# A four-layer graph attention kernel: layer 0's means and deviations made one batch ahead, on ACT and POOL

## The chip, the cores and the metric

The kernel runs on one core of a Trainium2 chip. The metric is the time of one execution on the device in microseconds. Before the change it is 2933.27 us, the median of three runs (2932.54 to 2933.4); the profiled execution spans 2931.4 us. Five engines work side by side, each with a queue of its own: TensorE (PE; its weight loads are listed as PEld), VectorE (DVE), ScalarE (ACT), GpSimd (POOL) and SyncE (SP, which here issues transfers).

## The reference

There are 16 batches; each is a graph of 1024 nodes with 256 features in fp32 and an adjacency matrix. Four layers follow one another, each on the output of the one before. Every layer starts with a layer norm over the features of each node and a relu, and then computes graph attention with a residual:

```python
def _layernorm(x, axis=-1, eps=1e-5):
    m = jnp.mean(x, axis=axis, keepdims=True)
    v = jnp.var(x, axis=axis, keepdims=True)
    return (x - m) / jnp.sqrt(v + eps)
```

Layers 0 to 2 have one head of 256 features: the normed and rectified features are multiplied by a matrix W, each edge gets a leaky-relu score from two dot products with a vector a, the scores are masked by the adjacency and put through a softmax, and the features of the neighbours are summed with these weights. Layers 1 and 2 pass the sum through an elu. Layer 3 has four heads of 64 features and a layer norm of its own inside each head.

For the change only the first step of layer 0 matters: the mean and the deviation of the 256 features of each input node. They depend on the input x alone.

## The kernel before

**Tiles.** A batch's features lie in SBUF as a tile x_b of 128 partitions by 8 node tiles by 256 features. The eight node tiles are treated in four pairs. In the listing P is 128, NI is 8, D is 256, B is 16 and HALF is 512.

**From features to V.** `project` (L315) makes one pair ready for the attention. It needs the means and the reciprocal deviations. Batch 0's layer 0 takes them from DVE's bn_stats. All others have sums of the features: DVE turns a sum into a negative mean (L332), subtracts it and rectifies (L302), ACT squares the difference and adds the squares up (L309), and POOL adds a constant (L292) and raises to the power −1/2 (L293). PE transposes the centred features into a psum tile "misc" (L338; there are two such tiles), ACT copies them out as hT (L340; three buffers), PE multiplies them by W into an accumulator (L345), and an `evict` function scales the result by the reciprocal deviation into V (ACT at L413 and L415 or L433 and after, DVE at L417). In layers 1 to 3 the sums come for free from the residual addition before; in layer 0 the function `first` (L512) lets DVE sum the features up first (L517).

**Attention, layers 0 to 2.** `attend` runs it. `weigh` puts a row of scores on all partitions with PE (L374), and DVE makes eight tiles of edge weights from it (L367, one fused operation over 128 by 1024). `product` multiplies weights by V, eight matmuls of 257 columns for a node tile (L461). `finish` divides by the total (DVE L385 and L386), for layers 1 and 2 with an elu of two ACT passes (L393 and L395) and two DVE additions (L396 and L397), and the next layer's `project` follows for each pair.

**Layer 3.** For each of four heads, `weigh3` makes rows of scores (PE L574) and weights (DVE L367), and PE forms the sums and totals in blocks of 24 matmuls with 32-column operands (L586). ACT copies the two accumulators out (L663), PE transposes them (L670 and L678), DVE divides (L681), and `center` and `rescale` do the head's layer norm over POOL (L544, L561 and L562), DVE (L545 to L551, L555 and L560) and ACT (L553), again with POOL's L292 and L293. At each of the eight copies L663 one further step of two side tasks is taken: `next(testing)`, a check of the adjacency by ACT (L175), and `next(coming)`, the load of the batch two ahead.

**The load.** `load` (above L146) fetches the adjacency as bytes on POOL's queue. It then issues four transposing transfers of the mask on SP's queue, and after these the transfer of the 1 MB of x, also on SP's queue. x_b has three buffers.

**What sets the order.** Each batch is a Python generator; even batches form one stream, odd batches another, and a small loop runs the two with weights given by the `yield` values, so that one batch's layer 3 is interleaved with layers 1 and 2 of the other stream's batch. Within what this emits, a list scheduler sets the order of each engine's queue from estimated costs; instructions put under `tc.keep_in_program_order` keep their order among themselves. An engine then takes its queue as built.

Of the kernel before, what the change touches and what calls it, by code (L numbers as in the profile page):

```python
# [32 lines left out]
F32 = mybir.dt.float32  # L33
BF = mybir.dt.bfloat16
# [3 lines left out]
AF = mybir.ActivationFunctionType  # L38
ALU = mybir.AluOpType
AX = mybir.AxisListType  # L40

P = 128
# [3 lines left out]
LN_EPS = 1e-5  # L46
# [15 lines left out]
def short_path(ctx: ExitStack, tc: tile.TileContext, ins: dict, out: bass.AP, bad: bass.AP):  # L62

    nc = tc.nc
    x, adj = ins["x"], ins["adj"]
    B, N, D = x.shape
    H, T, E = ins["L3_a_src"].shape
    NI = N // P
# [19 lines left out]
    minus_half = const.tile([P, 1], F32, name="minus_half")  # L88
# [21 lines left out]
    xs, masks = {}, {}  # L110
# [3 lines left out]
    def fetch_nodes(b: int):  # L114
        xs[b] = nodes.tile([P, NI, D], F32, name="x_b")
        if b == 0:

            for c in range(NI // 2):
                nc.scalar.dma_start(
                    xs[b][:, ts(c, 2), :],  # L120
                    x[b, ts(c, 2 * P), :].rearrange("(p t) f -> p t f", t=2),
                )
            return
        fetch = nc.sync.dma_start(xs[b].rearrange("p (c t) f -> p c t f", t=2), in_blocks(x[b]))
        if b > 0:
            tc.keep_in_program_order(fetch)

    def load(b: int):


        narrow = narrows[b % 2]
        rows = narrow.bitcast(U8)
        if b == 0:

            for h in range(NH):
                for t in range(2):
                    cast = nc.gpsimd.dma_start(
                        halves[h].bitcast(U8).rearrange("(c t q) j -> t c q j", t=2, q=P)[t],
                        adj[b].rearrange("(c q t) j -> t c q j", t=2, q=P)[t, :, :, ts(h, HALF)],
                    )  # L140
                    tc.keep_in_program_order(cast)
        else:
            for c in range(NI // 2):
                cast = nc.gpsimd.dma_start(
                    rows.rearrange("(c t q) j -> c q t j", t=2, q=P)[c],
                    adj[b, ts(c, 2 * P), :].rearrange("(q t) j -> q t j", t=2),  # L146
                )
                tc.keep_in_program_order(cast)
        if b < 2:
            fetch_nodes(b)  # L150
        yield

        mask = masks[b] = nodes.tile([P, NI // 2, N, 2], U8, name="mask")
        for c in range(NI // 2):
            turn = nc.sync.dma_start_transpose(
                mask[:, c].rearrange("p n t -> p (n t)").bitcast(BF),
                halves[c // NH][:, ts(c % NH, P)] if b == 0 else narrow[:, ts(c, P)],
            )
            tc.keep_in_program_order(turn)
            yield  # L160
        if b > 1:
            fetch_nodes(b)
            yield

    def test(b: int):
# [17 lines left out]
    work = ctx.enter_context(tc.tile_pool(name="work", bufs=3))  # L183
# [6 lines left out]
    bias = const.tile([P, D], F32, name="bias")  # L190
# [98 lines left out]
    def inverse_root(squared: bass.AP, n: int, elements: int, eps: float, times=1.0) -> bass.AP:  # L289

        r = small.tile([P, max(n, NI) if n > 2 else n], F32, name=f"rstd{8 if n > 2 else n}")[:, :n]
        nc.gpsimd.tensor_scalar(r, squared, times, elements * eps, op0=ALU.mult, op1=ALU.add)  # L292
        nc.gpsimd.tensor_tensor(r, r, minus_half.to_broadcast([P, n]), op=ALU.pow)  # L293
        return r
# [1 line left out]
    def accumulator(b: int) -> bass.AP:  # L296
        return psum.tile([P, HALF], F32, name=f"acc{b % 2}")

    def center_by_sums(xb: bass.AP, minus_mean: bass.AP, pair: int, centered: bass.AP) -> bass.AP:

        for n in range(2):
            nc.vector.tensor_scalar(  # L302
                centered[:, n, :], xb[:, 2 * pair + n, :], minus_mean[:, n : n + 1], 0.0,
                op0=ALU.add, op1=ALU.max,
            )
        squared = small.tile([P, 2], F32, name="squared")
        for n in range(2):
            square = work.tile([P, D], BF, name="square", bufs=1)
            nc.scalar.activation(  # L309
                square, xb[:, 2 * pair + n, :], AF.Square, bias=minus_mean[:, n : n + 1],  # L310
                accum_out=squared[:, n : n + 1],
            )
        return inverse_root(squared, 2, D, LN_EPS)

    def project(b: int, l: int, xb: bass.AP, sums: bass.AP, pair: int, evict):  # L315


        centered = work.tile([P, 2, D], F32, name="centered", bufs=3)
        if sums is None:
            mv = small.tile([P, 2, nc.vector.BN_AGGR_DIM], F32, name="mv", bufs=2)  # L320
            for n in range(2):
                stats = small.tile([P, nc.vector.BN_STATS_DIM], F32, name="stats", bufs=1)
                nc.vector.bn_stats(stats, xb[:, 2 * pair + n, :])
                nc.vector.bn_aggr(mv[:, n, :], stats)
                nc.vector.tensor_scalar(  # L325
                    centered[:, n, :], xb[:, 2 * pair + n, :], mv[:, n, 0:1], 0.0,
                    op0=ALU.subtract, op1=ALU.max,
                )
            rstd = inverse_root(mv[:, :, 1], 2, D, LN_EPS, D)
        else:  # L330
            minus_mean = small.tile([P, 2], F32, name="minus_mean")
            nc.vector.tensor_scalar_mul(minus_mean, sums[:, ts(pair, 2)], -1.0 / D)  # L332
            rstd = center_by_sums(xb, minus_mean, pair, centered)
        yield 0.5
        turned = psum.tile([P, NK, 2 * P], F32, name="misc")
        for n in range(2):
            for k in range(NK):
                nc.tensor.transpose(turned[:, k, ts(n, P)], centered[:, n, ts(k, P)], ident)  # L338
        hT = wide.tile([P, NK, 2 * P], F32, name="hT", bufs=3)
        nc.scalar.mul(hT, turned, ROOT_D)  # L340
        yield 1.0
        for n in range(2):
            projected = accumulator(b)[:, : D + EXT[l]]
            for k in range(NK):
                nc.tensor.matmul(  # L345
                    projected, hT[:, k, ts(n, P)], W[l][:, k, :],
                    start=(k == 0), stop=(k == NK - 1),
                )
            evict(2 * pair + n, projected, rstd[:, n : n + 1])
        yield 2.5  # L350
# [48 lines left out]
        )  # L399

    def batch(b: int):
        xb = xs.pop(b)
        if b == 0:
            next(preparing)
        coming = load(b + 2) if b + 2 < B else iter(())
# [21 lines left out]
        def begin3():  # L427
            h3 = last["h3"] = single.tile([P, NI, D], F32, name="h3")
            V3 = nodes.tile([P, NI, H, E + 1], F32, name="V", bufs=4)
            ex = last["ex"] = small.tile([P, NI, 3 * H], F32, name="ex", bufs=2)  # L430

            def evict3(i: int, projected: bass.AP, rstd: bass.AP):
                nc.scalar.activation(ex[:, i, :], projected[:, D:], AF.Exp, scale=rstd)  # L433
                nc.scalar.mul(h3[:, i, :], projected[:, :D], rstd)
                q = ex[:, i, :H].unsqueeze(2)
                nc.gpsimd.tensor_mul(
                    V3[:, i, :, :E], h3[:, i, :].rearrange("p (h e) -> p h e", h=H),
                    q.to_broadcast([P, H, E]),
                )
                nc.gpsimd.tensor_copy(V3[:, i, :, E:], q)  # L440
                nc.gpsimd.tensor_add(xb[:, i, :], xb[:, i, :], beta)  # L441

            return V3, evict3
# [63 lines left out]
            add_elu(xb[:, i, :], acc, total)  # L507

        V, evict = begin(0)
        sums = small.tile([P, NI], F32, name="sums_of_x")  # L510

        def first(pair: int):  # L512
            if b == 0:

                yield from project(b, 0, xb, None, pair, evict)
                return
            nc.vector.tensor_reduce(sums[:, ts(pair, 2)], xb[:, ts(pair, 2), :], AX.X, ALU.add)  # L517
            yield from project(b, 0, xb, sums, pair, evict)

        pairs = [first(pair) for pair in range(NI // 2)]  # L520
        for n in range(NI // 2 + 2):
            for pair in range(max(n - 2, 0), min(n + 1, NI // 2)):
                yield from islice(pairs[pair], 1)
# [82 lines left out]
        def add_totals(h: int, j: int):  # L606
# [4 lines left out]
            ]  # L611
            in_tiles(parts, total, j == 2, j == NI - 4)

        behind = weigh3(0)
        yield from start(behind, b)

# [7 lines left out]
        for h in range(H):  # L624
# [36 lines left out]
            for accT in (acc, total) if h == 0 else (total, acc):  # L661
                copies.append(wide.tile([P, HALF], F32, name="sums"))
                nc.scalar.copy(copies[-1], accT)  # L663
                next(testing)
                next(coming, None)
            sums, totals = copies if h == 0 else copies[::-1]
            yield 0.5
            turned = psum.tile([P, NG, P], F32, name="misc")
# [26 lines left out]
            else:  # L695
                normed += [center(h, slice(g * NG, g * NG + NG), nc.vector) for g in range(NH)]
            yield 1.0
        for _ in coming:
            pass
        while normed:  # L700
            rescale(*normed.pop(0), engine=nc.vector if len(normed) == 0 and b == B - 1 else nc.gpsimd)
# [403 lines left out]
```

## Time and profile before

| | before |
|---|---|
| time, median of three | 2933.27 us |
| PE busy | 2810.0 us (96%) |
| DVE busy | 2147.9 us (73%) |
| ACT busy | 1088.2 us (37%) |
| POOL busy | 981.3 us (33%) |
| granted clock of PE in the steady windows | 1.00 |
| start, steady part, end (cuts at 242 and 2741 us) | PE busy 216.5 of 242, 2442.2 of 2499, 151.2 of 191 us |

The busy share of an engine is the time in which it carries out instructions, as a share of the span. The steady part repeats every 178.5 us or so, once for each batch; the windows and timelines below are taken from one such period, from 1134.84 to 1313.40 us, in which one batch is in layers 3 and then 0 and the other in layers 1 and 2. In a timeline a row starts with its start and its length in us, and a bracket at its end tells how long the engine was idle before it and what ended that. In the profile the records of an fp32 matmul appear twice, so that a group of 24 matmuls L586 is shown as x48.

### The profile page before, as it was taken

To read this page: it belongs to the slowest core of one execution; us is meant where nothing else is said; L and a number is where in the kernel's file an instruction comes from. 1 tells how busy PE (TensorE), PEld (TensorE's weight loads), DVE (VectorE), ACT (ScalarE), POOL (GpSimd) and SP (SyncE) were. 2 spreads that over 40 slices of the span, in tenths; PEclk is the share of its full clock that TensorE was granted. 3 is DMA by queue.
4 is the path that set the end of the run, shared out by engine and by line. 5 is a ranking of instruction groups with operands and counts; after the bars stand their busy time and mean duration, and the time that the engine had idled before them with its cause. 6 is when DMAs were issued, how large, how long until landed. Compare 5 with 4: busy or idle time off the path is not lost.

```text
span 2931.4 us, 44756 instructions
## 1 busy us (share of the span) xinstructions
PE 2810.0 (96%) x16790; PEld 1961.9 (67%) x16790; DVE 2147.9 (73%) x4490; ACT 1088.2 (37%) x3010; POOL 981.3 (33%) x1533
## 2 busy tenths in 40 slices
PE   7999999999999999999999999999999999999986
PEld 5775857668576685766758577685766857667552
DVE  5658688586976859778586885868768587685857
ACT  1333434343343433424334343433434334343332
POOL 2123324243242423424233242432424224242333
PEclk9999999999999999999999999999999999999998
DMA  8204022030321303122031220303203031110101
GB/s 126 39 8 65 30 30 58 8 51 29 37 51 16 56 17 51 37 29 59 1 51 37 30 58 8 51 30 37 51 12 47 29 49 39 15 30 1 22 22 31
DMA packets 127967, 106.14 MB, mean 36 GB/s; under 512 B 79872, under 2 KB 98432, under 8 KB 127744
## 3 DMA queue, kind: packets, MB, share of 16 engines
q0 software_dynamic: 47328, 66.10, 15.4%
q1 hardware_dynamic: 79568, 35.53, 5.4%
q8 instruction: 135, 2.21, 0.3%
q10 hardware_dynamic: 848, 1.57, 0.2%
q14 instruction: 88, 0.72, 0.1%
HBM read 153.49 MB, written 33.55 MB: 64 GB/s over the span
## 4 chain that ended last, share of the span: by engine, by line
PE 59%; DVE 26%; issue 8%; POOL 3%; ACT 3%; DMA 0%; POOLq 0%; ACTq 0%; SPq 0%; DVEq 0%
PE acc L461 36%; DVE weights L367 16%; PE acc L586 10%; PE acc L345 9%; PE misc L338 2%; DVE centered L302 2%; POOL rstd L293 2%; DVE V L417 1%; PE row L374 1%; POOL y L544 1%; DVE y L545 1%; DVE var L555 1%; ACT square L309 1%; DVE y L551 1%; DVE mean L549 1%
## 5 line engine op out<-in xcount | busy, mean ns | idle before, releaser
L461 PE MATMUL acc<-V,weights 128*128 128x257 f32 x6144 | 1435.6, 384 | 33.5 <-DVE weights L367 15.7
L461 PEld LDWEIGHTS acc<-V,weights 128*128 128x128 f32 x6144 | 1136.6, 190 | 281.9 <-DVE weights L367 75.3
L586 PE MATMUL acc<-weights,V 128*32 128x512 f32 x6144 | 691.7, 596 | 12.0 <-DVE weights L367 8.1
L367 DVE SCALAR_TENSOR_TENSOR weights<-row,ex,mask 128x1024 f32<-128x1024 f32 x512 | 629.0, 1272 | 97.3 <-PE row L574 65.8
L345 PE MATMUL acc<-W,hT 128*128 128x259 f32 (+1 forms) x2048 | 516.1, 389 | 38.1 <-ACT hT L340 26.9
L367 DVE SCALAR_TENSOR_TENSOR weights<-row,V,mask 128x1024 f32<-128x1024 f32 x384 | 473.7, 1273 | 0.8 <-PE row L374 0.8
L345 PEld LDWEIGHTS acc<-W,hT 128*128 128x128 f32 x2048 | 378.7, 190 | 135.1 <-ACT hT L340 44.4
L586 PEld LDWEIGHTS acc<-weights,V 128*32 128x32 f32 x6144 | 189.1, 110 | 417.7 <-issue 410.3
L393 ACT ACTIVATE below<-acc,inv 128x256 f32<-128x256 f32 x256 | 121.1, 473 | 813.1 <-DVE inv L386 569.6
L293 POOL TENSOR_TENSOR rstd<-rstd,minus_half 128x2 f32<-128x2 f32 (+1 forms) x321 | 292.8, 912 | 20.3
L309 ACT ACTIVATE square<-x_b,minus_mean 128x256 bf16<-128x256 f32 x504 | 255.7, 507 | 110.3 <-DVE minus_mean L332 105.3
L441 POOL TENSOR_TENSOR x_b<-x_b,beta 128x256 f32<-128x256 f32 x128 | 93.5, 731 | 488.6 <-ACT square L309 483.5
L292 POOL TENSOR_SCALAR rstd<-squared 128x2 f32<-128x2 f32 x252 | 80.0, 317 | 464.0 <-ACT square L309 451.0
L385 DVE TENSOR_SCALAR inv<-acc 128x1 f32<-128x1 f32 x256 | 39.1, 153 | 255.3 <-PE acc L461 254.0
L302 DVE TENSOR_SCALAR centered<-x_b,minus_mean 128x256 f32<-128x256 f32 x504 | 195.7, 416 | 5.1
L340 ACT ACTIVATE hT<-misc 128x512 f32<-128x512 f32 x256 | 150.2, 592 | 129.6 <-PE misc L338 129.3
L396 DVE SCALAR_TENSOR_TENSOR x_b<-below,x_b 128x256 f32<-128x256 f32 x256 | 131.8, 515 | 84.9 <-ACT below L393 83.0
L663 ACT COPY sums<-acc 128x512 f32<-128x512 f32 x128 | 74.9, 585 | 308.6 <-PE acc L586 301.0
L413 ACT ACTIVATE V<-acc,rstd 128x3 f32<-128x3 f32 x384 | 98.4, 261 | 231.1 <-PE acc L345 230.6
L417 DVE TENSOR_SCALAR V<-acc,rstd,V 128x256 f32<-128x256 f32 x256 | 131.4, 537 | 59.8 <-ACT V L413 58.9
L338 PE MATMUL misc<-ident,centered 128*128 128x128 f32 x1024 | 158.7, 277 | 13.7 <-DVE centered L325 11.5
L170 POOL DMA_DIRECT2D adj_i<-in_adj_dram x128 | 74.4, 582 | 290.1 <-ACT adj_i L175 248.8
(96 smaller groups left out, 2212.8 us busy)
## 6 DMA issues: line engine op xcount, KB each, us to landing
adj_i<-in_adj_dram POOLq DMA_DIRECT2D x128, 256.0 KB, 3.9
x_b<-in_x_dram SPq DMA_DIRECT2D x15, 1024.0 KB, 6.4
narrow<-in_adj_dram POOLq DMA_DIRECT2D x60, 256.0 KB, 9.3
out_dram<-y POOLq DMA_DIRECT2D x30, 512.0 KB, 7.5
x_b<-in_x_dram ACTq DMA_DIRECT2D x4, 256.0 KB, 6.1
narrow_half<-in_adj_dram POOLq DMA_DIRECT2D x4, 256.0 KB, 16.9
mask<-narrow SPq DMA_TRANSPOSE x60, 3.7
weights<-in_L_gnn_a_dram SPq DMA_DIRECT2D x3, 256.0 KB, 5.5
```

Source lines behind the costliest of these rows:

```text
L293: nc.gpsimd.tensor_tensor(r, r, minus_half.to_broadcast([P, n]), op=ALU.pow)
L302: nc.vector.tensor_scalar(centered[:, n, :], xb[:, 2 * pair + n, :], minus_mean[:, n : n + 1], 0.0, op0=ALU.add, op1=ALU.max,)
L309: nc.scalar.activation(square, xb[:, 2 * pair + n, :], AF.Square, bias=minus_mean[:, n : n + 1], accum_out=squared[:, n : n + 1],)
L338: nc.tensor.transpose(turned[:, k, ts(n, P)], centered[:, n, ts(k, P)], ident)
L340: nc.scalar.mul(hT, turned, ROOT_D)
L345: nc.tensor.matmul(projected, hT[:, k, ts(n, P)], W[l][:, k, :], start=(k == 0), stop=(k == NK - 1),)
L367: nc.vector.scalar_tensor_tensor(w, r, c(j), masks[b][:, j // 2, :, j % 2], op0=op, op1=ALU.mult)
L393: nc.scalar.activation(below, acc[:, :D], AF.Exp, scale=inv)
L396: nc.vector.scalar_tensor_tensor(xi, below, 1.0, xi, op0=ALU.min, op1=ALU.add)
L417: nc.vector.tensor_scalar(V[:, i, :D], projected[:, :D], rstd, V[:, i, D : D + 1], op0=ALU.mult, op1=ALU.mult,)
L461: nc.tensor.matmul(accs[i], weights[j][:, ts(i, P)], V[:, j, : D + 1], start=(j == 0), stop=(j == NI - 1),)
L586: made = nc.tensor.matmul(accT[ts(n, QUAD), :], values, moving, start=first, stop=last)
```

## The change

Layer 0's statistics depend on x alone, so they can be made as soon as x is there. The change makes them in layer 3 of the batch two ahead (the same stream), where ACT and POOL have room:

- `norm_ahead(b)` makes, for each of the four pairs, the totals of the features (two ACT Identity passes with an accumulated sum), the negative means (POOL), and the accumulated squares of the differences (two ACT Square passes). At the end it makes all eight reciprocal deviations at once (two POOL operations). It has eight steps, and one is taken at each copy L663. Batch 1's are made at once when its stream begins; batch 0 keeps bn_stats.
- `project` gets a branch that uses these values: it only subtracts and rectifies (`relu_centered`, the part of `center_by_sums` that was at L302). `first` with its L517 goes, and so do L332, L309, L292 and L293 of layer 0.
- x must be there earlier: `load` fetches x ahead of the mask's transposing transfers, with one more step between, and layer 3 takes one step of `coming` at its start.
- The tile `ex` goes from two buffers to one, to make space.

```diff
@@ load
-        if b < 2:
-            fetch_nodes(b)
+        if b > 1:
+            yield
+        fetch_nodes(b)
         yield
...
             tc.keep_in_program_order(turn)
-            yield
-        if b > 1:
-            fetch_nodes(b)
             yield
...
+    def norm_ahead(b: int):
+
+        totals = small.tile([P, NI], F32, name="totals_of_x", bufs=1)
+        minus_mean = small.tile([P, NI], F32, name="minus_means", bufs=2)
+        squared = small.tile([P, NI], F32, name="squares_of_x", bufs=1)
+        for pair in range(NI // 2):
+            for i in (2 * pair, 2 * pair + 1):
+                square = work.tile([P, D], BF, name="square", bufs=1)
+                tc.keep_in_program_order(
+                    nc.scalar.activation(
+                        square, xs[b][:, i, :], AF.Identity, accum_out=totals[:, i : i + 1]
+                    )
+                )
+            nc.gpsimd.tensor_scalar_mul(
+                minus_mean[:, ts(pair, 2)], totals[:, ts(pair, 2)], -1.0 / D
+            )
+            yield
+            for i in (2 * pair, 2 * pair + 1):
+                square = work.tile([P, D], BF, name="square", bufs=1)
+                tc.keep_in_program_order(
+                    nc.scalar.activation(
+                        square, xs[b][:, i, :], AF.Square, bias=minus_mean[:, i : i + 1],
+                        accum_out=squared[:, i : i + 1],
+                    )
+                )
+            yield
+        rstd = small.tile([P, NI], F32, name="first_rstd", bufs=2)
+        nc.gpsimd.tensor_scalar_add(rstd, squared, D * LN_EPS)
+        nc.gpsimd.tensor_tensor(rstd, rstd, minus_half.to_broadcast([P, NI]), op=ALU.pow)
+        norms_ahead[b] = minus_mean, rstd
...
@@ project
+        elif isinstance(sums, tuple):
+            minus_mean, rstd = (a[:, ts(pair, 2)] for a in sums)
+            relu_centered(xb, minus_mean, pair, centered)
         else:
...
     def batch(b: int):
+        if b == 1:
+            for _ in norm_ahead(b):
+                pass
         xb = xs.pop(b)
+        ahead = norm_ahead(b + 2) if b + 2 < B else iter(())
...
-            ex = last["ex"] = small.tile([P, NI, 3 * H], F32, name="ex", bufs=2)
+            ex = last["ex"] = small.tile([P, NI, 3 * H], F32, name="ex", bufs=1)
...
-        sums = small.tile([P, NI], F32, name="sums_of_x")
-
-        def first(pair: int):
-            if b == 0:
-
-                yield from project(b, 0, xb, None, pair, evict)
-                return
-            nc.vector.tensor_reduce(sums[:, ts(pair, 2)], xb[:, ts(pair, 2), :], AX.X, ALU.add)
-            yield from project(b, 0, xb, sums, pair, evict)
-
-        pairs = [first(pair) for pair in range(NI // 2)]
+
+        known = None if b == 0 else norms_ahead.pop(b)
+        pairs = [project(b, 0, xb, known, pair, evict) for pair in range(NI // 2)]
...
+        next(coming, None)
         behind = weigh3(0)
...
                 next(testing)
                 next(coming, None)
+                next(ahead, None)
...
-        for _ in coming:
+        for _ in chain(coming, ahead):
             pass
```

More of the change, by code (lines that the diff above doesn't have):

```diff
@@ L297, in accumulator, with relu_centered @@
         return psum.tile([P, HALF], F32, name=f"acc{b % 2}")
-    def center_by_sums(xb: bass.AP, minus_mean: bass.AP, pair: int, centered: bass.AP) -> bass.AP:
+    def norm_ahead(b: int):
[27 more added lines that the diff above has]
+        norms_ahead[b] = minus_mean, rstd
+    norms_ahead = {}
+    def relu_centered(xb: bass.AP, minus_mean: bass.AP, pair: int, centered: bass.AP):
         for n in range(2):
@@ L305, in center_by_sums @@
             )
+    def center_by_sums(xb: bass.AP, minus_mean: bass.AP, pair: int, centered: bass.AP) -> bass.AP:
+        relu_centered(xb, minus_mean, pair, centered)
         squared = small.tile([P, 2], F32, name="squared")
@@ L329, in project @@
             rstd = inverse_root(mv[:, :, 1], 2, D, LN_EPS, D)
+        elif isinstance(sums, tuple):
+            minus_mean, rstd = (a[:, ts(pair, 2)] for a in sums)
+            relu_centered(xb, minus_mean, pair, centered)
         else:
```

## The prediction

> **What bounds the kernel now.** I read the busy table first, then the chain of waits.
>
> ```profile
> PE 2810.0 (96%) x16790; PEld 1961.9 (67%) x16790; DVE 2147.9 (73%) x4490; ACT 1088.2 (37%) x3010; POOL 981.3 (33%) x1533
> ...
> PE 59%; DVE 26%; issue 8%; POOL 3%; ACT 3%; DMA 0%; POOLq 0%; ACTq 0%; SPq 0%; DVEq 0%
> ```
>
> TensorE is busy 96%; ACT and POOL, which take over the work, are mostly idle. Then the windows of one steady period (one batch finished, 178.56 us), whole and cut where layer 0 of the next batch begins (columns: window, length, busy time and count of each engine, clock, DMA share, GB/s):
>
> ```profile
> 1134.84:1313.40 178.56, 174.56 (x1051) 122.51 (x1050) 133.46 (x277) 68.16 (x189) 61.57 (x95) 1.00 0.22 36
> 1134.84:1184.00 49.16, 49.16 (x339) 29.41 (x337) 40.11 (x81) 20.06 (x49) 16.97 (x20) 1.00 0.38 53
> 1184.00:1313.40 129.40, 125.40 (x713) 93.09 (x713) 93.35 (x197) 48.10 (x141) 44.60 (x75) 1.00 0.15 30
> ```
>
> PE waits 4.0 us in a period and **none of it in layer 3**, where the change puts its work. The waits of PE in that period (what waited, for whom, us, times, longest):
>
> ```profile
> PE acc L345 <- ACT hT L340: 1.7, 1, 1.7
> PE acc L461 <- DVE weights L367: 0.6, 1, 0.6
> PE acc L461 <- ACT above L395: 0.5, 1, 0.5
> PE acc L345 <- DVE V L417: 0.4, 1, 0.4
> PE acc L586 <- DVE inverses L385: 0.3, 1, 0.3
> PE acc L345 <- ACT above L395: 0.2, 1, 0.2
> ```
>
> The first, fourth and last stand where layer 0 begins, together 2.2 us: what the change can win. The largest, by the timeline of PE (start, length, engine, line, operation, count, and the wait before it):
>
> ```profile
> 1194.13 0.70 PE L345 MATMUL acc<-W,hT 128*128 128x259 f32 x2 [1.67 <-ACT hT L340]
> ```
>
> and in the timeline of ACT the two copies of hT that it waits for, at the end of twelve squares that stand nearly back to back:
>
> ```profile
> 1193.50 1.06 ACT L340 ACTIVATE hT<-misc 128x512 f32<-128x512 f32 x2
> ```
>
> **What the skill says.** "TensorE: Matmul & The Clock Gate", section "Architectural detail: the array is 16× 32×32, not 1× 128×128": ACT, DVE and GpSimd take their queues strictly in order. The trace agrees: the copy at 1193.50 starts when the square before it ends, though its input was ready. "ScalarE: Activation LUTs", section "Table sets: the hidden batching unit": identity is in every table set, so the new Identity passes should load none; before has one table load, and Exp and Square alternate in it. "SBUF — State Buffer", section "SBUF: two separate sides": DVE and GpSimd lock each other out of a port pair. The trace agrees: L302 took 1.47 us at 1187.68, beside POOL's L544, against 0.34 at 1189.67.
>
> **The change, part by part.** The prices (columns: line, engine, operation, output and input, count, busy us, mean ns, idle before):
>
> ```profile
> L309 ACT ACTIVATE square<-x_b,minus_mean 128x256 bf16<-128x256 f32 x504 | 255.7, 507 | 110.3 <-DVE minus_mean L332 105.3
> ...
> L293 POOL TENSOR_TENSOR rstd<-rstd,minus_half 128x2 f32<-128x2 f32 x256 | 187.1, 731 | 14.9
> ...
> L293 POOL TENSOR_TENSOR rstd<-rstd,minus_half 128x8 f32<-128x8 f32 x63 | 103.7, 1646 | 5.2
> ...
> L332 DVE TENSOR_SCALAR minus_mean<-sums_of_x 128x2 f32<-128x2 f32 x252 | 45.1, 195 | 4.0
> ...
> L517 DVE TENSOR_REDUCE sums_of_x<-x_b 128x2 f32<-128x512 f32 x60 | 40.1, 671 | 0.0
> ```
>
> *DVE:* 60 L517 and 60 L332 go: 60 × (0.671 + 0.195) = 52 us, 3.5 a period. *POOL:* 60 pairs of add (0.317) and pow (0.731) go, −63 us; 60 small multiplications at about 0.25 and 15 adds and pows of eight (0.2 + 1.65) come, +43. POOL is idle two thirds of the time; its 20 us are off the path. *ACT:* 120 Identity come. No row shows one: below, the skill's price ("What ACT_TABLE_LOAD costs", same page as the tables) of 186 ns + 0.833 ns per element, 0.40 us for 256; above, the square's 0.51; each with a 0.19 read of the accumulator. I take the square's pitch of 0.62, 8 × 0.62 = 5 us a period. With the 120 moved squares 16 × 0.62 = 10 us enter the layer-3 stretch, where ACT is busy 20 of 49 us. By sums all this fits. *Transfers:* x goes ahead of the mask turns, which start later by its issue. It lands in 6.4 us and is read some 80 us later: nothing. *ex* in one buffer: its last reader lies some 60 us ahead of its next writer: nothing.
>
> **What the sums leave out is the order.** A list scheduler sets each queue, and with less work on DVE and more on ACT it sets it otherwise. The built order of the changed kernel shows the same 11,146 PE instructions, but in layer 3 in another sequence. Before (from the timeline of PE):
>
> ```profile
> 1146.60 5.36 PE L586 MATMUL acc<-weights,V 128*32 128x512 f32 x48
> 1151.89 0.66 PE L678 MATMUL misc<-ident,sums 128*128 128x128 f32 x4
> 1152.38 1.92 PE L345 MATMUL acc<-W,hT 128*128 128x259 f32 x8
> 1154.23 5.36 PE L586 MATMUL acc<-weights,V 128*32 128x512 f32 x48
> 1159.52 3.73 PE L461 MATMUL acc<-V,weights 128*128 128x257 f32 x16
> ```
>
> After: L678, L345 and L461 stand **ahead of** the first of these L586 blocks, and the second block comes only after two L461 blocks. The order before put 5.3 us of independent work between a producer and PE's next need of it. I walked the new order with the trace's start times and durations:
>
> 1. L678 now reaches PE at 1146.5. It writes a psum tile "misc", of which there are two, and the other must have been read by L340. In ACT's new order L340 follows two squares (end 1143.05), two Identity (1144.3), POOL's multiplication (1144.65), two Squares that wait for it (1146.0), L393 and L395: it ends near 1147.3. PE waits **+0.8** (0.5 to 1.0). Everything on PE queues behind.
> 2. Some 17 us on, the second L345 of a pair needs an accumulator that L395 frees. L395 stands behind DVE's L386, and that behind four L367 (1.27 each), L555, L396, L397 and L560; ahead of it on ACT also stand two Squares. L386 comes at about 1163.6, L395 ends near 1165.15, PE arrives at about 1164.2: **+1.0** (0 to 2.5).
> 3. Layer 0: the waits of 1.7, 0.4 and 0.2 go. But in DVE's new queue the first L367 of layer 0 stands behind L560, which waits for POOL's pow of 1.65 us. Before, one L367 stood in front of that wait:
>
> ```profile
> 1195.22 0.69 DVE L560 TENSOR_TENSOR y<-y,rstd 128x512 f32<-128x512 f32 x1 [0.84 <-POOL rstd L293]
> ```
>
> L461 needs all eight weights tiles. The eighth is ready 26.9 us after the last L586 block by my walk, 26.5 before; so the 2.2 us won reappear as a wait for weights: net **+0.3** (−1 to +1).
>
> Sum +2.05 a period (0.8 + 1.0 + 0.3, rounded down); 14 batches have a successor in their stream: 14 × 2.05 = 29 us.
>
> 4. Start: batch 1's statistics are made at once when its stream begins, so 16 passes × 0.62 = 10 us of ACT and a pow stand in front of its first evictions L413, which stood at 112.85 to 118 in before. PE has batch 0's layer 0 only in part to fill that: **+5** once (2 to 7).
>
> 2933.3 + 29 + 5 = **2967 us**.
>
> **Rivals.** *Faster*: the scheduler's order is harmless, as real releases come earlier than my walk (steps 1 and 2 hang on differences under 1 us), and DVE's 3.5 us carry the weights forward. The 2.2 us of waits go: 14 × −2.2 = −31, about **2902**. For it: DVE is second on the chain with 26%, and the weights are its longest term. Against: PE waits nowhere in layer 3 now, so each new wait there is pure loss. *Wash*: only step 3's gain is real (−2.2) and 1 and 2 cost about as much (+1.8), with a small loss at the start: about **2933**. *Worse*: steps 1 and 2 at their upper ends, 1.0 + 2.5 + 1.0 = 4.5 a period, +63 and the start's 5: about **3001**.
>
> **Chances.** As walked (2945 to 2985) 0.57, worse 0.10, faster 0.25, wash 0.08. Range: 2905 to 2990, leaving a tenth at each end: the faster case's lower part, and most of worse. Chances of faster, same, slower: 0.25, 0.08, 0.67, the wash taken as the same.
>
> **What would show it.** Step 1: in the waits of PE a line L678 for ACT hT L340 near 0.8 us in each period. Step 2: L345 for ACT above L395 near 1 us in layer 3. Step 3: L345 for hT gone where layer 0 begins, and the first L461 waits for weights L367 longer than 0.6. Step 4: the time to 242 us longer by about 5. A layer-3 stretch that stays at about 49 us with PE never idle would refute 1 and 2, and then the time falls below 2933. Identity above 0.51 us, or a second table load, would refute the price of ACT.

## The result, and the profile after

The changed kernel takes **2978.87 us** (median of five runs, 2977.86 to 2980.39) against 2933.4 us before (2932.54 to 2934.81): a ratio of 1.0155, 95% interval 1.014 to 1.017. It is 45.5 us slower. The prediction was 2967 us in a range of 2905 to 2990, slower with a chance of 0.67.

Line numbers moved. In the changed kernel L306 is the new Identity, L310 the negative means on POOL, L317 the new Square, L324 and L325 the reciprocal deviations. Of the old lines, L292 and L293 became L290 and L291, L302 L332, L309 L343, L340 L378, L345 L383, L367 L405, L385 and L386 L423 and L424, L393 and L395 L431 and L433, L461 L503, L555 L589, L560 L594, L574 L608, L586 L620, L670 and L678 L706 and L714, and the adjacency check L175 and its fetch L170 L173 and L168.

The page of the changed kernel, busy table and chain of waits:

```profile
PE 2829.0 (95%) x16790; PEld 1973.2 (66%) x16790; DVE 2110.5 (71%) x4370; ACT 1149.0 (39%) x3250; POOL 941.8 (32%) x1503
...
PE 52%; DVE 27%; issue 9%; ACT 6%; POOL 5%; DMA 1%; POOLq 0%; ACTq 0%; SPq 0%; DVEq 0%
```

The work moved as intended: DVE 37 us less, POOL 40 less, ACT 61 more. Yet PE, which has the same work, is on the chain for 52% of the time in place of 59%, and ACT and POOL, which were at 3% each, are on it for 6% and 5%.

Where did the time go? The two profiled executions lie 47.2 us apart (2978.6 and 2931.4 us). The fetch of the next x stands on SP's queue once per batch, always just after the last POOL operation that frees its buffer, so its start is a mark that all kernels share. In before the marks are 178.54 us apart (mean from the fourth to the fifteenth), in after 180.93: **+2.39 a period**, 26 us over these eleven. The fourth mark comes at 503.11 in place of 485.33: **+17.8 at the start**. The rest behind the last mark is 3 us.

PE's waits between the fourth and the fifteenth mark, eleven periods, in the changed kernel (what waited, for whom, us in all, times, longest):

```profile
PE acc L503 <- DVE weights L405: 29.1, 24, 2.0
PE acc L383 <- ACT hT L378: 7.6, 11, 0.7
PE acc L503 <- ACT above L433: 5.8, 11, 0.8
PE acc L383 <- ACT above L433: 5.7, 22, 0.3
PE misc L714 <- ACT hT L378: 4.9, 10, 0.5
PE acc L620 <- DVE inverses L423: 2.9, 11, 0.3
```

The same eleven periods of before had 6.5 us for weights, 18.3 for hT, 4.1 for V, and 2.2 for the elu in front of L345. So the wait for hT fell by a full microsecond a period, the one for V went, and the one for weights grew by two. New in layer 3 are L714 and half of the L383 waits. The timeline of PE shows where they stand in one period:

```profile
1173.31 0.56 PE L608 MATMUL row<-thirds_T,rows_of 96*128 96x128 bf16 x7
1174.38 0.66 PE L714 MATMUL misc<-ident,sums 128*128 128x128 f32 x4 [0.52 <-ACT hT L378]
...
1191.91 1.15 PE L383 MATMUL acc<-W,hT 128*128 128x259 f32 x4 [0.33 <-ACT above L433]
...
1221.75 2.02 PE L383 MATMUL acc<-W,hT 128*128 128x259 f32 x8 [0.69 <-ACT hT L378]
1225.77 1.13 PE L503 MATMUL acc<-V,weights 128*128 128x257 f32 x4 [2.00 <-DVE weights L405]
```

In front of L714 there is no block of 24 L620 any more; it follows the L608 rows directly and waits. And where layer 0 begins, PE reaches the first L503 early and waits 2.00 us. The timeline of DVE tells for what:

```profile
1221.09 0.69 DVE L589 TENSOR_REDUCE var<-wide 128x8 f32<-128x512 f32 x1 [0.24 <-ACT wide L587]
...
1223.83 0.69 DVE L594 TENSOR_TENSOR y<-y,rstd 128x512 f32<-128x512 f32 x1 [1.60 <-POOL rstd L291]
1224.43 3.66 DVE L405 SCALAR_TENSOR_TENSOR weights<-row,V,mask 128x1024 f32<-128x1024 f32 x3
...
1228.92 6.04 DVE L405 SCALAR_TENSOR_TENSOR weights<-row,V,mask 128x1024 f32<-128x1024 f32 x5
```

All eight weights of layer 0 now stand behind the wait for POOL's pow. Before, one of them ran ahead of it.

### The profile page after: what moved, and what is told of

The parts are those of the page before. It is cut to its first block, busy times and chain, and to the rows that moved or that the text cites. A ratio compares the mean times of both kernels' runs of the same rounds, so it can differ in the third digit from the quotient of the medians.

```text
span 2978.6 us, 44694 instructions
## 1 busy us (share of the span) xinstructions
PE 2829.0 (95%) x16790; PEld 1973.2 (66%) x16790; DVE 2110.5 (71%) x4370; ACT 1149.0 (39%) x3250; POOL 941.8 (32%) x1503
## 4 chain that ended last, share of the span: by engine, by line
PE 52%; DVE 27%; issue 9%; ACT 6%; POOL 5%; DMA 1%; POOLq 0%; ACTq 0%; SPq 0%; DVEq 0%
PE acc L503 31%; DVE weights L405 17%; PE acc L620 9%; PE acc L383 9%; POOL y L578 2%; PE misc L376 2%; ACT square L343 2%; POOL rstd L291 2%; DVE y L579 1%; DVE x_b L435 1%; ACT below L431 1%; DVE x_b L434 1%; DVE var L589 1%; DVE y L585 1%; DVE mean L583 1%
## 5 line engine op out<-in xcount | busy, mean ns | idle before, releaser
L503 PE MATMUL acc<-V,weights 128*128 128x257 f32 x6144 | 1439.2, 386 | 61.2 <-DVE weights L405 43.5
L503 PEld LDWEIGHTS acc<-V,weights 128*128 128x128 f32 x6144 | 1143.3, 191 | 309.3 <-DVE weights L405 98.6
L620 PE MATMUL acc<-weights,V 128*32 128x512 f32 x6144 | 691.7, 596 | 11.5 <-DVE weights L405 7.6
L405 DVE SCALAR_TENSOR_TENSOR weights<-row,ex,mask 128x1024 f32<-128x1024 f32 x512 | 630.5, 1274 | 96.1 <-PE row L608 64.6
L383 PE MATMUL acc<-W,hT 128*128 128x259 f32 (+1 forms) x2048 | 516.8, 392 | 28.8 <-ACT hT L378 13.9
L405 DVE SCALAR_TENSOR_TENSOR weights<-row,V,mask 128x1024 f32<-128x1024 f32 x384 | 472.9, 1274 | 1.6 <-PE row L412 1.6
L620 PEld LDWEIGHTS acc<-weights,V 128*32 128x32 f32 x6144 | 188.6, 110 | 421.1 <-issue 415.0
L383 PEld LDWEIGHTS acc<-W,hT 128*128 128x128 f32 x2048 | 381.4, 192 | 127.5 <-ACT above L433 25.2
L431 ACT ACTIVATE below<-acc,inv 128x256 f32<-128x256 f32 x256 | 121.3, 474 | 705.1 <-DVE inv L424 476.6
L343 ACT ACTIVATE square<-x_b,minus_mean 128x256 bf16<-128x256 f32 x384 | 195.2, 508 | 151.2 <-DVE minus_mean L370 140.7
L291 POOL TENSOR_TENSOR rstd<-rstd,minus_half 128x2 f32<-128x2 f32 (+2 forms) x261 | 248.3, 952 | 16.3
L423 DVE TENSOR_SCALAR inv<-acc 128x1 f32<-128x1 f32 x256 | 39.4, 154 | 292.5 <-PE acc L503 291.3
L378 ACT ACTIVATE hT<-misc 128x512 f32<-128x512 f32 x256 | 151.0, 596 | 190.5 <-PE misc L376 190.2
L290 POOL TENSOR_SCALAR rstd<-squared 128x2 f32<-128x2 f32 x192 | 37.8, 197 | 478.8 <-ACT square L343 469.3
L376 PEld LDWEIGHTS misc<-ident,centered 128*128 128x128 f32 x1024 | 122.7, 144 | 61.7 <-issue 19.0
L173 ACT ACTIVATE adj_i<-adj_i,minus_half 128x1024 bf16<-128x1024 bf16 x128 | 147.3, 1151 | 18.5 <-DMA adj_i<-in_adj_dram 18.5
L168 POOL DMA_DIRECT2D adj_i<-in_adj_dram x128 | 76.0, 594 | 237.7 <-ACT adj_i L173 214.2
L435 DVE SCALAR_TENSOR_TENSOR x_b<-above,x_b 128x256 f32<-128x256 f32 x256 | 122.1, 477 | 18.6 <-ACT hT L378 0.9
```

Of the source, the lines that this page charges most:

```text
L173: square = nc.scalar.activation(adj_i, adj_i, AF.Square, bias=minus_half, accum_out=squares[:, b, i : i + 1])
L343: nc.scalar.activation(square, xb[:, 2 * pair + n, :], AF.Square, bias=minus_mean[:, n : n + 1], accum_out=squared[:, n : n + 1],)
L383: nc.tensor.matmul(projected, hT[:, k, ts(n, P)], W[l][:, k, :], start=(k == 0), stop=(k == NK - 1),)
L405: nc.vector.scalar_tensor_tensor(w, r, c(j), masks[b][:, j // 2, :, j % 2], op0=op, op1=ALU.mult)
L431: nc.scalar.activation(below, acc[:, :D], AF.Exp, scale=inv)
L435: nc.vector.scalar_tensor_tensor(xi, above, 0.0, xi, op0=ALU.add, op1=ALU.add, accum_out=total)
```

## The experiments

Two theories. **Order** (mine): the new work has room, but with other loads the scheduler builds other queues, and these cost. **Load**: the new passes on ACT, or the transfers moved, cost by themselves. All runs are set beside the kernel before in the same session (2933.6, 2934.4 and 2933.6 us); the two right-hand columns are from the profiled run.

| run | time, us | period, us | 4th mark, us |
|---|---|---|---|
| before | 2933.4 | 178.54 | 485.3 |
| changed | 2978.9 | 180.93 | 503.1 |
| e1 side edits alone | 2933.6 | 178.54 | 487.7 |
| e2 new work added, unused | 2946.8 | 178.48 | 500.0 |
| e3 old work removed, no new work | 2971.4 | 180.84 | 491.5 |
| e4 changed, old sums kept as dead work | 2960.3 | 179.49 | 499.9 |
| e5 changed, batches 1 and 2 the old way | 2963.4 | 180.83 | 487.0 |
| e6 changed, last y times rstd on POOL | 2943.9 | 178.28 | 501.6 |
| e7 before, last y times rstd on POOL | 2910.6 | 177.03 | 484.3 |
| e8 changed, three repairs | 2911.7 | 177.04 | 485.8 |
| e9 changed, start's L310 on DVE | 2973.1 | 180.92 | 496.5 |
| e10 changed, batch 1 the old way | 2973.7 | 180.81 | 496.3 |
| e11 changed, e5 and e6 together | 2925.9 | 178.24 | 487.1 |

**e1, the side edits alone.** The edit is before with the moved fetch, the further step of the load at the start of layer 3, and `ex` in one buffer.

```diff
-        if b < 2:
-            fetch_nodes(b)
+        if b > 1:
+            yield
+        fetch_nodes(b)
...
-            ex = last["ex"] = small.tile([P, NI, 3 * H], F32, name="ex", bufs=2)
+            ex = last["ex"] = small.tile([P, NI, 3 * H], F32, name="ex", bufs=1)
...
+        next(coming, None)
         behind = weigh3(0)
```

> The kernel before with only the side edits: x fetched ahead of the mask's turns, ex in one buffer; nothing made ahead. Order theory (mine): transfers and ex are hidden, so 2933, within 3 us. Transfer rival: the earlier fetch or the later mask turns delay layer 0 or the masks; then a good part of the 45 us is here, 2950 or more.

2933.56 us, ratio 1.000 (0.9991 to 1.0009). These edits are free, and the transfer rival is out.

**e2, the new work without its use.** Before plus e1 plus `norm_ahead` as in the change; layer 0 ignores what it makes.

```diff
+        ahead = norm_ahead(b + 2) if b + 2 < B else iter(())
...
                 next(coming, None)
+                next(ahead, None)
```

> The kernel before plus the side edits plus all of the new work on ACT and POOL, whose results nobody uses; layer 0 still makes its own statistics the old way. The built queue of PE in the steady periods is that of the kernel before. Order theory: ACT has room, PE's independent block L586 still covers it; about +0 to +0.5 us a period and 2 to 7 at the start: 2935 to 2947. Load rival (the new passes delay hT and the elu wherever they stand): +1 to +2 a period at least, 2955 or more, near the 2979 of the changed kernel.

2946.81 us, ratio 1.0043 (1.0027 to 1.006), at the upper edge of what order allowed. Sixteen more ACT passes a period, and the period is 178.48 against 178.54: in the steady part the load costs **nothing**. PE's first waits there, over eleven periods, are those of before:

```profile
PE acc L376 <- ACT hT L371: 18.1, 11, 1.7
PE acc L496 <- DVE weights L398: 6.6, 11, 0.6
```

All of its 13 us lie ahead of the fourth mark, which is 14.6 us late, at least twice the 2 to 7 us expected for the start.

**e3, the old work removed without the new.** `norm_ahead` hands out two constant tiles.

```diff
-        totals = small.tile([P, NI], F32, name="totals_of_x", bufs=1)
...
-        norms_ahead[b] = minus_mean, rstd
+        yield
+        norms_ahead[b] = fixed
```

> The changed kernel without any of the new work: the negative means of layer 0 are a constant 0 and the reciprocal deviations a constant 1/16 for batches 1 to 15 (the statistics are left out). The built queue of PE is the new one of the changed kernel. Order theory: the queue of PE and DVE costs even with less work everywhere: L714 no longer waits (that needs the ACT passes too, -0.5 a period and its after-effects), but the second projection's wait for the elu and the wait for weights behind L594 stay: +1 to +1.7 a period, 2948 to 2960. Load rival: with 3.5 us of DVE and 10 us of ACT a period taken away and nothing put in, it is faster than before: 2900 to 2930.

2971.39 us, ratio 1.0127 (1.011 to 1.0144): slower than before by 38 us, **with less work on three engines and more on none** (two small constants, written once, apart). The direction is order's, the size beyond it: I had expected L714's wait to go with the ACT passes. It does not. Its period is 2.30 us longer than before, nearly all of the changed kernel's 2.39. The timelines of e3 (there L691 is L714, L355 is hT's copy, L408 the first elu pass, L382 the weights), of DVE, ACT and PE in turn:

```profile
1156.87 2.46 DVE L382 SCALAR_TENSOR_TENSOR weights<-row,ex,mask 128x1024 f32<-128x1024 f32 x2
...
1159.43 0.16 DVE L401 RECIPROCAL inv<-inv 128x1 f32<-128x1 f32 x1
```

```profile
1159.69 0.47 ACT L408 ACTIVATE below<-acc,inv 128x256 f32<-128x256 f32 x1 [2.67 <-DVE inv L401]
1160.06 0.47 ACT L410 ACTIVATE above<-acc,inv 128x256 f32<-128x256 f32 x1
1160.42 0.60 ACT L355 ACTIVATE hT<-misc 128x512 f32<-128x512 f32 x1
```

```profile
1161.07 0.66 PE L691 MATMUL misc<-ident,sums 128*128 128x128 f32 x4 [0.51 <-ACT hT L355]
```

ACT sits idle for 2.67 us, because the elu pass ahead of the copy waits for a reciprocal, and that stands behind two weights tiles on DVE. In the changed kernel the same idle time is filled with the Identity and Square passes, which end at 1172.99, when the reciprocal is ready too (L424 ends at 1172.90). Two arms end together; my walk saw one of them.

**e4, useless work put back.** The changed kernel, with the old sums computed at their old place and thrown away.

```diff
+        sums = small.tile([P, NI], F32, name="sums_of_x")
+        def first(pair: int):
+            if b > 0:
+                nc.vector.tensor_reduce(sums[:, ts(pair, 2)], xb[:, ts(pair, 2), :], AX.X, ALU.add)
+                unused = small.tile([P, 2], F32, name="minus_mean")
+                nc.vector.tensor_scalar_mul(unused, sums[:, ts(pair, 2)], -1.0 / D)
+            yield from project(b, 0, xb, known, pair, evict)
-        pairs = [project(b, 0, xb, known, pair, evict) for pair in range(NI // 2)]
+        pairs = [first(pair) for pair in range(NI // 2)]
```

> The changed kernel plus the old sums of x on DVE (L517 and L332 of layer 0 in the kernel before: 0.87 us a pair) at their old place, with results nobody uses. The built queue of PE in layer 3 is that of the kernel before again; where layer 0 begins the first weights tile still stands behind the wait for POOL's pow. Order theory: useless work makes it faster: the waits of L714 for hT and of L383 for the elu in layer 3 go (-1.3 to -1.8 a period), the wait for weights at the start of layer 0 stays (+0.8 to +1.3): 2945 to 2962. Load rival: more work on DVE can only cost: 2979 or more.

2960.33 us, ratio 1.0088 (1.0071 to 1.0105). Adding 3.5 us of DVE work a period made the kernel 18.5 us **faster**; the period fell by 1.44. Its waits (eleven periods) have no line for L714 (L723 there) and fewer for the elu, while the wait for weights stays:

```profile
PE acc L503 <- DVE weights L405: 27.6, 23, 1.9
...
PE acc L383 <- ACT above L433: 2.5, 12, 0.5
```

**e5, the start.** Batches 1 and 2 by the old path; nothing is made ahead until batch 1 is in its own layer 3, and `first` is back for these two.

```diff
-        if b == 1:
-            for _ in norm_ahead(b):
-                pass
-        ahead = norm_ahead(b + 2) if b + 2 < B else iter(())
+        ahead = norm_ahead(b + 2) if 2 < b + 2 < B else iter(())
```

> The changed kernel, but batches 1 and 2 make layer 0's statistics the old way; so nothing is made ahead at batch 1's start and in batch 0's layer 3; from batch 3 on it is the changed kernel. Start theory: the 12 to 15 us that the changed kernel and the 'added work' kernel lose before 500 us come from ACT and POOL waiting in a ring there (the new POOL operation waits for ACT and holds back the fetch of adj_i behind it in POOL's queue, and ACT waits for that fetch): 2979 - 13 = 2966, 2961 to 2970, and ACT's wait for the adj_i transfer in 110 to 330 us back from 18.5 to about 8 us. Rival (the start pays for the new queue orders, not for the work): 2974 or more.

2963.39 us, ratio 1.0099 (1.0084 to 1.0115): 15.5 us come back, within the expected span, and the period is unchanged. This does not decide against the rival of the expectation, since the edit undoes two things: batch 2's old sums are back on DVE, and with them PE's old order in batch 0's layer 3. Other runs tell the two apart. At the fourth mark e2, with the new work and the old order, is 14.6 us late, e3, with the new order and no new work, is 6.2 us late, and the changed kernel 17.8. So the work alone is enough for most of the loss at the start, and the order has a smaller part in it. What the work does in batch 0's layer 3 of the changed kernel is told by the timelines of POOL and then ACT and PE:

```profile
262.72 0.33 POOL L310 TENSOR_SCALAR minus_means<-totals_of_x 128x2 f32<-128x2 f32 x1 [0.47 <-ACT square L306]
263.01 0.61 POOL L168 DMA_DIRECT2D adj_i<-in_adj_dram  x1
271.05 0.18 POOL L290 TENSOR_SCALAR rstd<-squared 128x2 f32<-128x2 f32 x1 [7.42 <-ACT square L343]
...
272.01 0.60 POOL L168 DMA_DIRECT2D adj_i<-in_adj_dram  x1
```

```profile
266.98 1.15 ACT L173 ACTIVATE adj_i<-adj_i,minus_half 128x1024 bf16<-128x1024 bf16 x1 [3.31 <-DMA adj_i<-in_adj_dram]
...
276.01 1.15 ACT L173 ACTIVATE adj_i<-adj_i,minus_half 128x1024 bf16<-128x1024 bf16 x1 [4.07 <-DMA adj_i<-in_adj_dram]
```

```profile
277.79 0.66 PE L714 MATMUL misc<-ident,sums 128*128 128x128 f32 x4 [2.70 <-ACT hT L378]
```

POOL's queue holds a fetch of adj_i, then L310, then the next fetch; in before the two fetches stood side by side. L310 waits for ACT's Identity, which stands behind ACT's check L173, which waits for the first of the fetches. So the second fetch starts only when the first has landed, and each turn of this ring adds one landing of about 4 us (issued at 263.01, checked from 266.98). The longest wait, at 276.01, follows from it at one remove: its fetch, at 272.01, stands behind POOL's old L290, which waits for ACT's old Squares L343, and these stand behind the late check of 266.98. The copy that L714 needs, at 277.16, stands behind the check of 276.01. In e5 ACT's wait for adj_i from 110 to 330 us is back at 8.2 us from 18.5 (8.1 in before).

**e9, the ring alone.** For batches 1 and 2, L310 on DVE; all passes stay.

```diff
-            nc.gpsimd.tensor_scalar_mul(
+            (nc.vector if b < 3 else nc.gpsimd).tensor_scalar_mul(
```

> The changed kernel, but for batches 1 and 2 the four small products that turn totals into negative means (L310) run on DVE in place of POOL; all else is as changed. Ring theory: POOL's queue no longer waits for ACT between two fetches of adj_i, so ACT's wait for the adj_i transfer falls from 18.5 to about 8 us between 110 and 330 us, and most of the 12 to 14 us of batch 0's layer 3 goes: 2966 to 2972. Rival (the sixteen ACT passes themselves hold up batch 0's layer 3): 2976 or more.

2973.05 us, ratio 1.0132 (1.0115 to 1.0149). ACT's wait in that stretch is even below that of before:

```profile
ACT adj_i L173 <- DMA adj_i<-in_adj_dram: 5.2, 3, 2.6
```

The ring is broken and 5.8 us return, a microsecond less than the expected span allows; so it is a part of the start but not most of it.

**e10, batch 1 alone.** Only the passes at the start of the odd stream are undone (with `first` back for batch 1).

```diff
-        if b == 1:
-            for _ in norm_ahead(b):
-                pass
```

> The changed kernel, but batch 1 alone makes layer 0's statistics the old way; batch 2's are made ahead in batch 0's layer 3 as changed. My prediction's step 4 (batch 1's passes in front of its evictions) is undone alone. By the traces so far it is the smaller part: waits of PE between 110 and 150 us from 6.5 back to 3.7, so 2974 to 2977. If step 4 as predicted were the whole start, 2964 to 2968.

2973.73 us, ratio 1.0139 (1.0122 to 1.0156): 5.1 us, just over the expected span, of which PE's waits from 110 to 150 us are 2.8 (6.5 to 3.7). Of the 15.5 us, batch 1 is 5.1 and the ring 5.8, if the two add. The other 4.6 were not separated; the new order in batch 0's layer 3, which e5 undoes too, is among them.

**e6, the wait for the pow.** The last rescale of a batch takes its first product to POOL, which makes the pow anyway.

```diff
-            nc.vector.tensor_mul(yh, yh, rstd.unsqueeze(2).to_broadcast(shape))
+            first.tensor_mul(yh, yh, rstd.unsqueeze(2).to_broadcast(shape))
...
-            rescale(*normed.pop(0), engine=nc.vector if len(normed) == 0 and b == B - 1 else nc.gpsimd)
+            rescale(*normed.pop(0), engine=nc.vector if len(normed) == 0 and b == B - 1 else nc.gpsimd, first=nc.gpsimd if b < B - 1 else nc.vector)
```

> The changed kernel, with the last rescale of a batch's layer 3 (y times rstd, L594) moved from DVE to POOL for all batches but the last, so that DVE's weights of layer 0 no longer stand behind the wait for POOL's pow; the layer-3 queue of PE stays the new one. Order theory: the wait of L503 for weights where layer 0 begins (2.0 us) goes for the most part, and the clock dips that follow it: -0.8 to -2 a period: 2950 to 2968. Rival (weights are late for another reason, or POOL's 1.27 us in place of 0.69 us delays others): 2975 to 2985.

2943.91 us, ratio 1.0033 (1.0021 to 1.0045): 35 us off the changed kernel, more than the 11 to 29 expected, 2.65 a period. The wait for weights is down from 29.1 us:

```profile
PE acc L383 <- ACT hT L378: 7.6, 11, 0.7
PE acc L503 <- DVE weights L405: 6.8, 12, 0.6
```

**e7, the same move in the kernel before.**

> The kernel before with the same move of the last y times rstd from DVE to POOL. There one weights tile already stood in front of that wait, and the first wait is PE's for hT (1.7 us): little to win, 2926 to 2935. If the wait for pow were a cost of its own in either kernel, it would fall by the 10 to 20 us that the same move brings in the changed kernel.

2910.59 us, ratio **0.9919** (0.9903 to 0.9934). My expectation failed: the move is worth 1.51 a period there too. It had counted PE's waits, and in before no wait of PE for weights stands where layer 0 begins. The loss shows on DVE, which makes the weights. The timelines of DVE and then PE, first in before:

```profile
1192.50 0.69 DVE L555 TENSOR_REDUCE var<-wide 128x8 f32<-128x512 f32 x1 [0.24 <-ACT wide L553]
...
1199.57 6.04 DVE L367 SCALAR_TENSOR_TENSOR weights<-row,V,mask 128x1024 f32<-128x1024 f32 x5
...
1206.64 1.91 PE L345 MATMUL acc<-W,hT 128*128 128x259 f32 x8
```

and then in e7:

```profile
1184.88 0.69 DVE L555 TENSOR_REDUCE var<-wide 128x8 f32<-128x512 f32 x1 [0.24 <-ACT wide L553]
...
1191.61 4.85 DVE L367 SCALAR_TENSOR_TENSOR weights<-row,V,mask 128x1024 f32<-128x1024 f32 x4
...
1197.49 1.91 PE L345 MATMUL acc<-W,hT 128*128 128x259 f32 x8
```

From the start of the variance sum of layer 3's last head (L555, L589 in the changed kernel) to the end of layer 0's eighth weights tile, and from there to PE's next block of projections, in the period shown of each kernel:

| | sum to eighth tile, us | of it DVE idle for the pow | product by rstd | to PE's next block |
|---|---|---|---|---|
| before | 13.11 | 0.84 | on DVE | 1.03 |
| changed | 13.87 | 1.60 | on DVE | 1.02 |
| e6 | 11.57 | 0 | on POOL | 1.03 |
| e7 | 11.58 | 0 | on POOL | 1.03 |
| e8 | 11.57 | 0 | on POOL | 1.03 |

These times are the same in all eleven periods to 0.02 us, but for PE's distance in the changed kernel, which is 1.72 in the five periods with a dip of PE's clock (last section). PE's next block follows the eighth tile at the same distance in all five kernels, so the pace here is DVE's. Before less e7 is 1.53, the idle time and the product, against 1.51 a period measured. Changed less e6 is 2.30, and the clock adds about 0.3 a period (0.69 in five of eleven), against 2.65 measured. The change made the pow 1.14 a period dearer (2.65 − 1.51), since the one tile that ran ahead of it no longer does.

**e8, three repairs together.** The changed kernel with e6, e5 and the dead sums (without the product of e4).

> The changed kernel with three repairs: unused sums of x on DVE (0.67 us a pair) that bring back PE's old queue in layer 3, the last y times rstd on POOL, and batches 1 and 2 the old way. Order theory: the three losses go, and what the change was made for is left: 0.3 to 1.5 us a period better than before: 2910 to 2930. Load rival (the new passes on ACT cost by themselves): 2945 or more.

2911.7 us, ratio **0.9922** (0.9908 to 0.9935). Nothing of the loss remains. But nothing of the gain does either: its period is 177.04, e7's is 177.03. PE's wait for hT, from e7 and then from e8:

```profile
PE acc L345 <- ACT hT L340: 18.4, 11, 1.7
```

```profile
PE acc L383 <- ACT hT L378: 7.5, 11, 0.7
```

One microsecond of the very wait that the change was made for is gone, and the period did not move by 0.05 us. The table tells why: in both kernels the eighth weights tile comes 11.6 us after the variance sum, and PE's next block 1.03 us after the tile. PE's wait for hT lies inside this stretch, and shortening it lets PE arrive earlier at work that DVE has not released yet. (e8 still does the unused sums; a kernel that keeps the old order without them was not run.) Of all these kernels e7 is the fastest, level with e8, and it needs one product of the kernel before moved and nothing made ahead.

**e11, two repairs.** e5 and e6 without the dead sums.

> The changed kernel with two repairs of three: the last y times rstd on POOL, and batches 1 and 2 the old way; the layer-3 queue of PE stays the new one. If the losses add up: the 2944 of the POOL move alone less the 14 to 16 of the start: 2927 to 2932, and 1.2 us a period above the version with all three repairs. If they hide one another: 2936 or more.

2925.88 us, ratio 0.9973 (0.9962 to 0.9984), a microsecond better than expected. The losses add up, and the period is 1.20 above e8's: the layer-3 order, as in e4 (1.44) and between e6 and e8 (1.24).

## Why the prediction was right, and where its steps were off

The loss in the steady part has two terms: layer-3 order 1.24 (e6 less e8) and pow 1.14 (e6 and e7), together 2.38 against 2.39 measured. That they close is no check by itself, because it follows from e7 and e8 being level. Other readings of the two are e4 (1.44) and e11 less e8 (1.20) for the order, and DVE's timelines with the clock (0.76 + 0.3) for the pow.

- **The mechanism**, that the queues' new order costs and not the load: right, by e2 (load alone, no cost in the steady part) against e3 (order alone, 2.30 of the 2.39 a period). What the order hangs on is DVE's old sums: e4 brings it back by dead work.
- **Step 1** (L714 for hT, +0.8): the wait is there with 0.5, in ten of eleven periods. Its cause was half wrong: the Identity and Square passes that I put ahead of the copy could be left out (e3) and the wait stayed, because the elu pass ahead of it waits for DVE.
- **Step 2** (second projection for the elu, +1.0): the wait is 0.33; the pair of projections takes 2.45 us from its first start to the next block (1190.54 to 1192.99) in place of 1.82 (1167.87 to 1169.69), so +0.6. Steps 1 and 2 together were predicted as 1.8 and measured as 1.20 to 1.44.
- **Step 3** (layer 0, net +0.3): 1.14, the term most under-sized in the steady part. The walk put the eighth weights tile at 26.9 us after the last L586 block; it came at 27.3 (1234.96 − 1207.66), against 26.5 in before. The rest is about 0.3 of clock, below, which the prediction did not have. The wait for hT did not go but shrank to 0.7, and the 0.2 for the elu stayed as it was: PE waits there for a pass of the layer before, which the change does not touch.
- **Step 4** (start, +5): batch 1's passes cost 5.1 (e10), as said. But the start as a whole cost 15.5, and I had no step for batch 0's layer 3, where the ring and the passes come on top. (The 15.5 contain one ordinary period's loss, about 2.4 by the mean of the later ones, which the prediction counted among its 14.) That is the largest part of the 12 us by which the forecast fell short.
- **Costs put at nothing**: the fetch and `ex`, right by e1. Identity took 0.42 us, near the lower bound of 0.40 estimated from the Trainium skill ("ScalarE: Activation LUTs", section "What ACT_TABLE_LOAD costs") and below the 0.51 that I used:

```profile
L306 ACT ACTIVATE square<-x_b 128x256 bf16<-128x256 f32 x120 | 50.3, 420 | 1.4
```

- **Sums and readings**: busy time fell by 37 us on DVE where the sum said 52, and by 40 on POOL where it said 20, since prices moved in rows that stay, for instance the remaining negative means (0.278 us each in place of 0.195) and POOL's adds (0.197 in place of 0.317). And not quite all of PE's 4.0 us lay outside layer 3: 0.3, in front of L586, stand at the start of the next one, and all kernels have them.
- **Luck**: that 2.05 a period came near 2.39 owes something to it. Steps 1 and 2 were too dear by about 0.5 and step 3 too cheap by 0.8, and these errors offset each other.
- **The rival "faster"** failed not only for the new waits. Its 2.2 us a period were never to be had: e8 has none of the losses left and is level with e7.

## What to carry to other kernels

Where a scheduler builds the queues, compare the built order before the sums: work taken from an engine with time to spare can move another engine's independent block out from between a producer and its consumer. Before moving work to shorten a wait, ask what the engine does next; a wait in front of work that another engine paces was worth nothing here. And keep an operation that waits for a third engine out of the queue of the engine that paces; the cost can be missing from the other engine's waits. One product moved from DVE to POOL was worth 24 us in the kernel before.

## What I had not expected of the hardware

In these traces PE's granted clock sometimes falls after a gap of some two microseconds. In the windows of the changed kernel (length, busy times and counts, clock, DMA share, GB/s), after the 2.00 us wait for weights:

```profile
1043.00:1045.00 2.00, 0.57 (x1) 0.48 (x2) 2.00 (x3) 0.00 (x0) 1.66 (x2) 0.87 0.00 0
1045.00:1047.00 2.00, 2.00 (x8) 1.61 (x7) 2.00 (x3) 0.00 (x0) 1.70 (x2) 0.50 0.00 0
1047.00:1049.00 2.00, 2.00 (x9) 1.66 (x9) 2.00 (x4) 0.35 (x1) 0.74 (x1) 0.77 0.50 148
```

PE runs at half its clock for about 3 us, and the four L503 records there take 2.06 us in place of 1.13. It does not follow each such gap: the period from 1162.70 us has the same wait and no dip. Periods with a dip are some 0.7 us longer (181.34 against 180.64). In the steady part, the six kernels that wait 1.9 or 2.0 us for weights (changed, e3, e4, e5, e9, e10) show such dips. The other seven, whose longest wait there is 1.7 us or less, show none; e6, which is the changed kernel without that wait, is one of them. The length is not all, though: in e1 a dip follows waits of 0.93 and 1.62 us, at 136 us, and before has the same two waits and no dip. The batch-0 stretch of the changed kernel has two dips (at 280 and 310 us), and they are part of the start's loss. What decides between dip and no dip was not tested.
